# Attention and mixture-of-LoRA block on one core: half of the probability tiles turned by VectorE squares and SBUF to SBUF DMAs instead of TensorE

## The chip, the cores and the metric

The kernel runs on one core of a Trainium2 chip. The metric is device time in microseconds (us) of one execution; lower is better. One execution with the hardware profiler gives the page and the trace that are quoted below.

## The reference

The input `x` has 4 sequences of 512 tokens with 1024 features, all in 32-bit floats. One transformer block is computed:

```python
x = x + layernorm(attention(layernorm(x)))          # 32 query heads, 8 key/value heads, 32 features each
x = x + layernorm(lora_moe(layernorm(x)))           # a dense 1024x1024 layer plus a top-2 mix of 8 LoRA experts

# attention, per head:
scores = q @ k.T / sqrt(32)                         # q, k after rotary embedding
scores = where(causal, scores, -1e20)
out = softmax(scores) @ v                           # then the output projection w_o
```

The change concerns the step between `softmax` and `@ v`. TensorE sums over partitions, so the probabilities, which are computed with queries on the partitions, have to be turned until the keys lie on the partitions.

## The kernel before

The 2048 tokens are cut into 16 tiles of 128 (`Tokens`; `tok.i` is the tile's place, 0 to 3, within its sequence). Dense layers work on pairs of tiles with seven block products in place of eight (`seven`): their weights come from HBM as pieces of 128x512 (`bring_pieces`, line 489) into a ring of `RING = 13` buffers, issued on SP's DMA queue. A piece is requested when the product that last used its buffer is done.

Attention of a tile is cut into groups (`Group`). A group takes four heads side by side on the TensorE array (`QUADS = 4`; `r` is the quadrant) and `n` columns of heads, so that `m = n * (i + 1)` blocks of 128 keys are handled at once: m is 4, 4, 3 and 4 for `i` = 0 to 3, with 2, 4, 8 and 8 groups per tile, 88 groups in all. For each group

- `scores` (TensorE, line 1390) writes all four quadrants to PSUM; VectorE adds the causal mask (line 1459) and takes the maxima (line 1469);
- `quadrant` lets ScalarE take the exponential (line 1411) into the SBUF tile `pr` and GpSimd (POOL) multiply by the reciprocal of the sum (line 1425);
- `turn` (line 1485) turns `pr` with TensorE, m squares of 128x128 per quadrant, into PSUM; `copy` (lines 335 and 336) brings them back to SBUF as `prT`, on ScalarE or VectorE, whichever the planner finds free;
- `values` (line 1508) multiplies `prT` with `v`; the result `av` is copied to `aT`.

The order of instructions on every engine is written out at build time by a planner, the class `Order`. Every piece of work is an `Op` with an estimated duration for each engine that could do it, or a TensorE `Step`; `_choice` picks TensorE's next step among the lanes (scores, turns, values, dense products), and `run` gives the other engines' work out in the planned order of time. The estimates are constants of the source. For DMAs, `sp(us, issue)` is the time that SP's queue is planned to be taken, and `LANDS = 2.8` us is added until the data is there. Once built, each engine keeps its order, and only semaphores delay it. SP's DMAs share eight semaphores in turn, so that an issue also waits for the DMA eight before it.

`Norm.apply` (lines 562 and 568) normalises rows on VectorE or ScalarE, and `load_y` (line 879) brings the residual rows.

Of the kernel before, what the change touches and what calls it, by code (L numbers as in the profile page):

```python
# [11 lines left out]
F32 = mybir.dt.float32  # L12
AF = mybir.ActivationFunctionType
ALU = mybir.AluOpType
AX = mybir.AxisListType

P = 128
# [4 lines left out]
EPS = 1e-5  # L22
MASKED = -1e30
QUADS = P // HD

# [64 lines left out]
class Order:  # L92
# [109 lines left out]
    def _choice(self, scores, values, lanes):  # L202

        later, ready, last = [], [], []
        score = scores[0] if scores else None


        value = values[0] if values and values[0].tiled else None
        waiting = []
        if score is not None and value is not None:  # L210
            if self._comes(score):
                waiting.append(values)
            if self._comes(value) and not self._is_ready(value):
                waiting.append(scores)
        for lane in lanes:
            at = self._ready(lane[0])
            if at is None:
                continue
            later.append(at)
            if at <= self.now:  # L220
                if any(lane is w for w in waiting):
                    last.append(lane)
                elif at + SAFE <= self.now:
                    return lane, None
                else:
                    ready.append(lane)
        if ready or last:
            return (ready + last)[0], None
        what = self._next()
        if what is not None:  # L230
            later.append(max(what[0], self.now + 1e-6))
        if not later:
            raise RuntimeError("TensorE's work cannot go on")
        return None, min(later)
# [31 lines left out]
def kernel(  # L266
# [24 lines left out]
    GL = E + E * R  # L291
    PSUM = bass.MemoryType.PSUM
    QSCALE = 1.0 / math.sqrt(HD)
    BANKS, SOFT, RING = 4, 8, 13

    const = ctx.enter_context(tc.tile_pool(name="const", bufs=1))
    xpool = ctx.enter_context(tc.tile_pool(name="xpool", bufs=1))
# [2 lines left out]
    qpool = ctx.enter_context(tc.tile_pool(name="qpool", bufs=8))  # L300
    kvpool = ctx.enter_context(tc.tile_pool(name="kvpool", bufs=4))
    soft = ctx.enter_context(tc.tile_pool(name="soft", bufs=SOFT))
    weights = ctx.enter_context(tc.tile_pool(name="weights", bufs=RING))
    small = ctx.enter_context(tc.tile_pool(name="small", bufs=2))
    ps_sc = ctx.enter_context(tc.tile_pool(name="ps_sc", bufs=1, space=PSUM))
# [4 lines left out]

    banks = Slots(BANKS)
    soft_slots, part_slots, piece_slots = Slots(SOFT), Slots(4), Slots(RING)
    xnT_slots, aT_slots, hT_slots = Slots(2), Slots(3), Slots(2)
    qT_slots, kT_slots, raw_slots, turn_slots = Slots(8), Slots(4), Slots(6), Slots(1)
    xa_slots, y_slots, w_slots, v_slots = Slots(1), Slots(3), Slots(4), Slots(8)
    order = Order(banks)
    start = order.start

# [12 lines left out]
    def copy(n, out, in_):  # L331

        return Op(
            0,
            act=(0.15 + n * 0.00085, lambda: nc.scalar.copy(out(), in_())),  # L335
            dve=(0.15 + n * 0.00105, lambda: nc.vector.tensor_copy(out(), in_())),  # L336
        )

    def combine(urgent, out, in0, in1, op, engines=("dve", "pool")):
# [155 lines left out]
    class Norm:  # L495
# [60 lines left out]
        def apply(self, dst, src, h):  # L556
            cols = slice(h * 512, (h + 1) * 512)
            yield Op(
                self.urgent,
                dve=(  # L560
                    0.66,
                    lambda: nc.vector.tensor_scalar(
                        dst()[:, cols], src()[:, cols], self.rstd, self.shift, ALU.mult, ALU.add
                    ),
                ),
                act=(
                    0.82,
                    lambda: nc.scalar.activation(  # L568
                        dst()[:, cols], src()[:, cols], AF.Identity, bias=self.shift, scale=self.rstd
                    ),  # L570
                ),
            )
# [299 lines left out]
    def load_y(tok):  # L872

        yield y_slots.take()
        yield has_rest if tok in pairs[0] else all_mixed

        def issue():
            tok.y = xpool.tile([P, D], F32, tag="y", bufs=3, name=f"y_{tok.t}")
            nc.sync.dma_start(out=tok.y, in_=x[tok.t * P : (tok.t + 1) * P, :])

        yield sp(P * D * 4 / 1024 / RATE, issue)
        yield LANDS
        tok.has_y.finish(order.at)
# [487 lines left out]
    class Group:  # L1371
        def __init__(self, tok, at, n):
            self.tok, self.seq, self.at, self.n = tok, tok.seq, at, n
            self.kt = at // GROUP
            self.name = f"{tok.t}_{at}"
            self.parts = 2
            self.exps, self.normed = [Task() for _ in range(QUADS)], [Task() for _ in range(QUADS)]
            self.rtot = [Task() for _ in range(QUADS // 2)]
            self.pr, self.prT = [None] * QUADS, [None] * QUADS
            self.has_prT = [Task() for _ in range(QUADS)]  # L1380

    def scores(g):

# [17 lines left out]

        def quadrant(r):
            urgent = 1 + r / QUADS
            yield soft_slots.take()
            pr = soft.tile([P, GROUP, P], F32, tag="soft", name=f"pr_{g.name}_{r}")
            pr = g.pr[r] = pr.rearrange("p a b -> p (a b)")
            for c in range(g.n):
                yield act(
                    0.5 + n * 0.00079,
                    urgent,  # L1410
                    lambda: nc.scalar.activation(  # L1411
                        pr[:, c * n : (c + 1) * n],
                        sc4[:, r, c, :],
                        AF.Exp,
                        bias=nmax[:, r, c : c + 1],
                        accum_out=total[:, r, c : c + 1],
                    ),
                )
            g.exps[r].finish(order.at)
            yield g.rtot[r // 2]  # L1420
            for c in range(g.n):
                yield pool(
                    0.33 + n * 0.00089,
                    urgent,
                    lambda: nc.gpsimd.tensor_scalar(  # L1425
                        pr[:, c * n : (c + 1) * n],
                        pr[:, c * n : (c + 1) * n],
                        rtot[:, r, c : c + 1],
                        1.0,
                        ALU.mult,  # L1430
                        ALU.mult,
                    ),
                )
# [42 lines left out]
        start(softmax(), order.now)  # L1476
        for h in range(QUADS // 2):
            start(totals(h), order.now)

    def turn(g, r):  # L1480

# [16 lines left out]
    def values(g):  # L1498
# [5 lines left out]
        for c in range(g.n):  # L1504
            for j in range(i + 1):
                for r in range(QUADS):
# [1 line left out]
                    nc.tensor.matmul(  # L1508
                        av[r * HD : (r + 1) * HD, c, :],
                        lhsT=g.seq.v[j][:, head * HD : (head + 1) * HD],  # L1510
                        rhs=g.prT[r][:, c * (i + 1) + j, :],
                        start=(j == 0),
                        stop=(j == i),
                    )

        def end():
            yield g.valued.done
            for r in range(QUADS):
                soft_slots.give(order.at)
            yield copy(  # L1520
                g.n * P, lambda: tok.aT[:, g.at : g.at + g.n, :], lambda: av[:, : g.n, :]
            )
# [83 lines left out]
    for k, g in enumerate(groups):  # L1606
# [4 lines left out]
        if k > 1:  # L1611
# [2 lines left out]
        g.turned = [  # L1614

            Step(0.109 * blocks, partial(turn, g, r), [g.normed[r | 1]], bank=True, turns=True)
            for r in range(QUADS)
        ]
        needs = [tok.seq.has_v[i] for i in range(tok.i + 1)] + [tok.aT_taken]
        g.valued = Step(0.218 * blocks, partial(values, g), needs, bank=True, soon=g.has_prT)  # L1620
# [133 lines left out]
```

## Time and profile before

| | us |
|---|---|
| median of 3 runs | 1164.1 (1162.73 to 1164.26) |
| profiled execution, its own time | 1164.45 |
| its span, first to last instruction | 1162.7 |
| granted TensorE clock | 0.996 of full speed |

| engine | busy us | instructions |
|---|---|---|
| TensorE, matmuls (PE) | 1136.4 | 7240 |
| TensorE, weight loads (PEld) | 624.5 | 7240 |
| VectorE (DVE) | 832.6 | 1629 |
| ScalarE (ACT) | 530.1 | 1545 |
| GpSimd (POOL) | 611.7 | 859 |

The span is the time from the first to the last instruction on the core. The chain of waits follows the work back from the last instruction, at each step to what released it, and is the view that tells which engine sets the end. Busy time of PE alone says little, for matmuls overlap. Issuing a DMA does not count as busy time: SP's queue (SPq) has rows of its own in the timeline. The DMA queue moved 230.12 MB in 117632 packets, and its packets took 60.7% of the time of 16 DMA engines.

### The profile page before, as it was taken

What the parts mean: (1) busy time and instruction counts of PE and PEld (TensorE: products, weight loads), DVE (VectorE), ACT (ScalarE), POOL (GpSimd) and SP (SyncE); (2) the same over time, 40 slices, a digit from 0 to 9 for tenths busy, and PEclk for the clock granted to TensorE, in tenths of its full rate; (3) what the DMA queues carried; (4) which work ended last, traced back from release to release, by engine and by line L of the source; (5) the groups of instructions that cost most, each with busy time, mean ns of one, the idle gap of its engine ahead of it and who ended that gap; (6) DMA issues with size and microseconds to landing.
All of it is one profiled execution on the core that took longest, in us unless ns stands there. A gap on an engine that the chain in (4) does not pass through costs nothing.

```text
span 1162.7 us, 21371 instructions
## 1 busy us (share of the span) xinstructions
PE 1136.4 (98%) x7240; PEld 624.5 (54%) x7240; DVE 832.6 (72%) x1629; ACT 530.1 (46%) x1545; POOL 611.7 (53%) x859
## 2 busy tenths in 40 slices
PE   7999999999999999999999999999999999999997
PEld 3455554655556455565555555456555555556443
DVE  4787767987678756787667876768866787668564
ACT  0354554555555355555434434455644555454010
POOL 2686856743756435544555253654545564547231
PEclk9999999999999999999999999999999999999999
DMA  9879777563773637625477443673457745585783
GB/s 349 277 255 310 248 253 263 170 220 97 257 239 96 199 109 253 192 83 176 141 244 256 137 135 118 219 229 106 149 168 233 243 135 160 164 268 187 221 285 118
DMA packets 117740, 231.48 MB, mean 199 GB/s; under 512 B 13440, under 2 KB 14464, under 8 KB 117632
## 3 DMA queue, kind: packets, MB, share of 16 engines
q1 hardware_dynamic: 117632, 230.12, 60.7%
q8 instruction: 58, 0.95, 0.3%
q14 instruction: 50, 0.41, 0.1%
HBM read 209.09 MB, written 20.97 MB: 198 GB/s over the span
## 4 chain that ended last, share of the span: by engine, by line
PE 86%; DVE 7%; DMA 3%; POOL 1%; ACT 1%; issue 1%; SPq 0%; POOLq 0%; ACTq 0%
PE acc_f L618 18%; PE acc_o L618 16%; PE acc_q L618 14%; PE pt_p L1485 11%; PE acc_kv L618 8%; PE sc L1390 7%; PE av L1508 6%; PE acc_gl L618 2%; DVE nmax L1469 2%; PE pt_xn L593 1%; PE pt_h L593 1%; DMA piece<-in_w_qkv_dram 1%; ACT pr L1411 1%; PE pt_q L1010 1%; DMA xa<-in_x_dram 1%
## 5 line engine op out<-in xcount | busy, mean ns | idle before, releaser
L1425 POOL TENSOR_SCALAR pr<-pr,rtot 128x256 f32<-128x256 f32 (+3 forms) x512 | 300.5, 602 | 251.9 <-DVE rtot L1440 183.3
L1411 ACT ACTIVATE pr<-sc,nmax 128x256 f32<-128x256 f32 (+3 forms) x512 | 265.0, 536 | 121.8 <-DVE nmax L1469 63.6
L1469 DVE TENSOR_REDUCE nmax<-sc 128x2 f32<-128x768 f32 (+3 forms) x176 | 198.2, 1126 | 33.7 <-ACT pr L1411 30.6
L1485 PEld LDWEIGHTS pt_p<-ident,pr 128*128 128x128 f32 x1280 | 144.5, 141 | 59.3 <-issue 49.1
L1485 PE MATMUL pt_p<-ident,pr 128*128 128x128 f32 x1280 | 173.2, 276 | 2.4 <-DVE raw_q L727 1.0
L335 ACT COPY prT<-pt_p 128x512 f32<-128x512 f32 (+1 forms) x261 | 134.1, 548 | 62.4 <-PE pt_p L1485 61.0
L1459 DVE TENSOR_TENSOR sc<-sc,cmask 128x256 f32<-128x256 f32 (+2 forms) x176 | 96.7, 550 | 48.6 <-PE sc L1390 39.0
L335 ACT COPY aT<-av 128x128 f32<-128x128 f32 (+2 forms) x83 | 26.1, 315 | 222.1 <-PE av L1508 222.0
L618 PE MATMUL acc_f<-piece,s_f 128*128 128x512 f32 x256 | 120.1, 602 | 2.1 <-DVE s_f L343 2.1
L618 PE MATMUL acc_kv<-wkv_sb,T_xn 128*128 128x512 f32 x256 | 119.4, 597 | 0.0
L1411 ACT ACTIVATION_READ_ACCUMULATOR pr<-sc,nmax 128x1 f32 x512 | 108.3, 212 | 0.0
L618 PE MATMUL acc_o<-piece,aT 128*128 128x512 f32 x232 | 105.9, 594 | 0.0
L618 PE MATMUL acc_q<-piece,s_q 128*128 128x512 f32 x224 | 105.4, 595 | 0.1
L618 PE MATMUL acc_q<-piece,T_xn 128*128 128x512 f32 x224 | 103.9, 594 | 0.1
L618 PE MATMUL acc_o<-piece,s_o 128*128 128x512 f32 x224 | 102.8, 593 | 0.0
L1390 PE MATMUL sc<-kT,qT 32*128 32x384 f32 (+3 forms) x1024 | 93.9, 464 | 0.5 <-ACT pr L1411 0.5
L1508 PEld LDWEIGHTS av<-prT,v 128*32 128x32 f32 x2560 | 64.8, 109 | 50.1 <-issue 35.0
L618 PE MATMUL acc_f<-piece,T_h 128*128 128x512 f32 x192 | 90.0, 592 | 0.0
L343 POOL TENSOR_TENSOR y<-y,w 128x512 f32<-128x512 f32 x61 | 79.1, 1309 | 20.3 <-ACT w L568 14.9
L1508 PE MATMUL av<-prT,v 128*32 128x128 f32 x2560 | 88.7, 276 | 0.2 <-DVE prT L336 0.2
L336 DVE COPY prT<-pt_p 128x512 f32<-128x512 f32 (+1 forms) x91 | 58.3, 642 | 31.3 <-PE pt_p L1485 29.7
L541 POOL TENSOR_TENSOR rstd<-veps,neg_half 128x1 f32<-128x1 f32 x64 | 35.0, 549 | 86.1 <-DVE veps L537 85.8
(154 smaller groups left out, 1416.3 us busy)
## 6 DMA issues: line engine op xcount, KB each, us to landing
piece<-mixed_f SPq DMA_DIRECT2D x128, 256.0 KB, 3.5
piece<-in_w_o_dram SPq DMA_DIRECT2D x116, 256.0 KB, 3.6
piece<-mixed_q SPq DMA_DIRECT2D x112, 256.0 KB, 3.4
piece<-mixed_o SPq DMA_DIRECT2D x112, 256.0 KB, 4.1
piece<-in_w_qkv_dram SPq DMA_DIRECT2D x100, 256.0 KB, 3.7
piece<-in_w_base_dram SPq DMA_DIRECT2D x96, 256.0 KB, 3.3
xa<-in_x_dram SPq DMA_DIRECT2D x32, 256.0 KB, 3.8
y<-in_x_dram SPq DMA_DIRECT2D x16, 512.0 KB, 5.7
```

Of the source, the lines that this page charges most:

```text
L335: act=(0.15 + n * 0.00085, lambda: nc.scalar.copy(out(), in_())),
L336: dve=(0.15 + n * 0.00105, lambda: nc.vector.tensor_copy(out(), in_())),
L343: engine.tensor_tensor(out=out(), in0=in0(), in1=in1(), op=op)
L541: nc.gpsimd.tensor_tensor(out=self.rstd, in0=self.veps, in1=neg_half, op=ALU.pow)
L618: nc.tensor.matmul(acc[0][:, :n], lhsT=lhsT(c), rhs=w(c), start=(c == 0), stop=last)
L1390: nc.tensor.matmul(sc[:, r, c * n : (c + 1) * n], lhsT=tok.qT[g.kt][rows, (g.at + c) % GROUP, :], rhs=seq.kT[g.kt][rows, :n], start=True, ...
L1411: lambda: nc.scalar.activation(pr[:, c * n : (c + 1) * n], sc4[:, r, c, :], AF.Exp, bias=nmax[:, r, c : c + 1], accum_out=total[:, r, c : ...
L1425: lambda: nc.gpsimd.tensor_scalar(pr[:, c * n : (c + 1) * n], pr[:, c * n : (c + 1) * n], rtot[:, r, c : c + 1], 1.0, ALU.mult, ALU.mult,),
L1459: lambda: nc.vector.tensor_tensor(out=diag, in0=diag, in1=cmask.unsqueeze(1).unsqueeze(1).to_broadcast([P, q, g.n, P]), op=ALU.add,),
L1469: lambda: nc.vector.tensor_reduce(nmax[:, some, : g.n], sc4[:, some], AX.X, ALU.max, negate=True),
L1485: nc.tensor.transpose(pt[:, j, :], g.pr[r][:, j * P : (j + 1) * P], ident)
L1508: nc.tensor.matmul(av[r * HD : (r + 1) * HD, c, :], lhsT=g.seq.v[j][:, head * HD : (head + 1) * HD], rhs=g.prT[r][:, c * (i + 1) + j, :], ...
```

## The change

Quadrants 0 and 1 (`TURNED = 2`) are turned as before. For quadrants 2 and 3 ScalarE writes the exponentials into a tile `pair` in which each row is cut into strips of 32 columns; VectorE turns every square of 32x32 in place with one instruction per group; 16 DMAs from SBUF to SBUF, each of 32 partitions, move the 4x4 grid of squares to their turned places in the tile `flat`; `values` reads `flat` for those quadrants. The planner is told 0.07 us of SP's queue for each of the 16.

Beside it, `copy` and `Norm.apply` go to ScalarE alone; the rings are smaller (`RING` 13 to 9, `SOFT` 8 to 6, `y` 3 to 2) to make room for two `pair` and two `flat` tiles; and one rule of `_choice`, which held scores back while values were about to come, is gone.

```diff
-            if self._comes(value) and not self._is_ready(value):
-                waiting.append(scores)
...
-    BANKS, SOFT, RING = 4, 8, 13
+    BANKS, SOFT, RING = 4, 6, 9
+    PAIRS, FLATS = 2, 2
+    SIDE = 32
+    NS = P // SIDE
...
     def copy(n, out, in_):
...
             act=(0.15 + n * 0.00085, lambda: nc.scalar.copy(out(), in_())),
-            dve=(0.15 + n * 0.00105, lambda: nc.vector.tensor_copy(out(), in_())),
...
         def apply(self, dst, src, h):
...
-                dve=(
-                    0.66,
-                    lambda: nc.vector.tensor_scalar(
-                        dst()[:, cols], src()[:, cols], self.rstd, self.shift, ALU.mult, ALU.add
-                    ),
-                ),
...
-            tok.y = xpool.tile([P, D], F32, tag="y", bufs=3, name=f"y_{tok.t}")
+            tok.y = xpool.tile([P, D], F32, tag="y", bufs=2, name=f"y_{tok.t}")
...
         def quadrant(r):
+            if r < TURNED:
+                yield soft_slots.take()
+                pr = soft.tile([P, GROUP, P], F32, tag="soft", name=f"pr_{g.name}_{r}")
+                pr = g.pr[r] = pr.rearrange("p a b -> p (a b)")
+                to = [pr[:, c * n : (c + 1) * n] for c in range(g.n)]
+                exp_in = [sc4[:, r, c, :] for c in range(g.n)]
+                exp_out = to
+            else:
+                yield g.has_pair
+                j = tok.i + 1
+                strips = g.pair[:, :, r - TURNED]
+                to = [strips[:, :, c * j : (c + 1) * j, :] for c in range(g.n)]
+                exp_in = [
+                    sc4[:, r, c, :].rearrange("p (j s k) -> p j s k", s=NS, k=SIDE)
+                    for c in range(g.n)
+                ]
+                exp_out = [a.rearrange("p s j k -> p j s k") for a in to]
...
+    def flip(g):
+        m = g.n * (g.tok.i + 1)
+        q = QUADS - TURNED
+        yield pair_slots.take()
+        g.pair = flips.tile([P, NS, q, m, SIDE], F32, tag="pair", bufs=PAIRS, name=f"pair_{g.name}")
+        g.has_pair.finish(order.at)
+        yield g.normed[TURNED:]
+        flat_pair = g.pair.rearrange("p s r m k -> p (s r m k)")
+        yield dve(
+            0.1 + NS * q * m * SIDE * 0.00105,
+            1,
+            lambda: nc.vector.transpose(out=flat_pair, in_=flat_pair),
+        )
+        yield flat_slots.take()
+        g.flat = flips.tile([P, NS, q, m, SIDE], F32, tag="flat", bufs=FLATS, name=f"flat_{g.name}")
+
+        def move():
+            for a in range(NS):
+                for b in range(NS):
+                    nc.sync.dma_start(
+                        out=g.flat[b * SIDE : (b + 1) * SIDE, a],
+                        in_=g.pair[a * SIDE : (a + 1) * SIDE, b],
+                    )
+
+        yield sp(NS * NS * 0.07, move, -1)
+        yield LANDS
+        pair_slots.give(order.at)
+        for r in range(TURNED, QUADS):
+            g.has_prT[r].finish(order.at)
...
     def values(g):
-                        rhs=g.prT[r][:, c * (i + 1) + j, :],
+                        rhs=(
+                            g.prT[r][:, c * (i + 1) + j, :]
+                            if r < TURNED
+                            else g.flat[:, :, r - TURNED, c * (i + 1) + j, :]
+                        ),
...
         g.turned = [
             Step(0.109 * blocks, partial(turn, g, r), [g.normed[r | 1]], bank=True, turns=True)
-            for r in range(QUADS)
+            for r in range(TURNED)
         ]
```

## The prediction

> **What bounds the kernel now.** I read the page's first section, then the chain that ended last, then that chain piece by piece in a stretch of dense work, then the waits and the issue rows of the DMA queue, since the change adds most of its instructions there.
>
> ```profile
> PE 1136.4 (98%) x7240; PEld 624.5 (54%) x7240; DVE 832.6 (72%) x1629; ACT 530.1 (46%) x1545; POOL 611.7 (53%) x859
> ...
> PE 86%; DVE 7%; DMA 3%; POOL 1%; ACT 1%; issue 1%; SPq 0%; POOLq 0%; ACTq 0%
> PE acc_f L618 18%; PE acc_o L618 16%; PE acc_q L618 14%; PE pt_p L1485 11%; PE acc_kv L618 8%; PE sc L1390 7%; PE av L1508 6%; PE acc_gl L618 2%; DVE nmax L1469 2%; PE pt_xn L593 1%; PE pt_h L593 1%; DMA piece<-in_w_qkv_dram 1%; ACT pr L1411 1%; PE pt_q L1010 1%; DMA xa<-in_x_dram 1%
> ```
>
> TensorE carries 86% of the chain; 11% is the turning of probabilities (pt_p). SP (SPq) carries nothing.
>
> ```profile
> 581.93 1.08 PE sc L1390 x16
> 583.01 1.01 PE av L1508 x32
> 584.02 1.02 PE pt_p L1485 x8
> 585.04 0.86 PE acc_f L618 x2
> 585.90 0.88 PE pt_p L1485 x8
> 586.78 6.87 PE acc_f L618 x16
> ```
>
> One group (four heads side by side on the array) is 1.08 us of scores, 1.01 of values and four turns of four squares, 0.44 each; everything else is dense products, 0.86 us for each 512-column product (two instructions).
>
> ```profile
> SPq L489 <- PE acc_q L618: 231.7, 167, 20.6
> SPq L489 <- PE acc_f L618: 224.2, 184, 10.9
> SPq L489 <- PE acc_o L618: 142.7, 174, 6.3
> ```
>
> Most of SP's waits are weight pieces waiting for TensorE to free a buffer: the queue runs ahead of its consumer and has time to spare.
>
> **What the change removes from TensorE.** Of 1280 squares, 640 stay. In the chain eight squares take 0.88 us, 0.11 each, so 640 x 0.11 = 70 us leave the engine that sets the end. The profiled execution took 1164.45 us around a span of 1162.7 and lies 0.35 us over the median of 1164.1. If nothing took the place of the squares: 1164.45 - 70 = 1094.
>
> **What it moves between VectorE and ScalarE.** VectorE loses its share of the copies (prT 58 us, T_h 14, kT 3, T_xn 10, lowT 2) and of the normalising passes (18 + 10 + 10): 126 us. It gains 88 square transposes of 1024 or 768 elements per partition. No row shows one; the nearest are the reductions over as many elements, 1.22 and 0.96 us: 56 x 1.22 + 32 x 0.96 = 99 us. As no row is a transpose I keep half of that and twice that as bounds, 50 and 200 us, and take 99, by the row; even 200 leaves VectorE at 900 us of work in a run that can't be under 1094. ScalarE loses 176 of the 352 prT copies and takes all that remain: 176 x about 0.55 = 97 us in place of 134, plus T_xn, T_h, kT and lowT (27 us) and 58 normalising passes of 0.81 (47 us): about +37 us, 49% busy. Both stay below TensorE, whose dense products cover them; without that cover they'd be worth tens of us at most. The exponentials and POOL's multiplications write the same elements in runs of 32; between nothing and 10% of 565 us on engines that are half idle, I take nothing.
>
> **What it adds to SP's queue.** Each of the 88 groups issues 16 DMAs of 32 partitions (24 or 32 KB): 1408 beside the 808 of before. They need a price per issue, and the planner in the kernel says 0.07 us (`sp(NS * NS * 0.07, ...)`). The trace's rows:
>
> ```profile
> 1.69 3.95 SPq L392 DMA_DIRECT2D wkv_sb<-in_w_qkv_dram  x8
> 5.96 0.33 SPq L489 DMA_DIRECT2D piece<-in_w_qkv_dram  x1
> 6.73 0.33 SPq L392 DMA_DIRECT2D bqkv_sb<-in_b_qkv_dram  x1
> 7.37 0.33 SPq L489 DMA_DIRECT2D piece<-in_w_qkv_dram  x1
> ...
> 11.38 0.33 SPq L489 DMA_DIRECT2D piece<-in_w_qkv_dram  x1
> ...
> L489 SPq DMA_DIRECT2D piece<-mixed_f x128: 319/320/853, 234.2 to 1141.2; - x128
> ...
> L879 SPq DMA_DIRECT2D y<-in_x_dram x16: 328/333/497, 19.3 to 1111.1; - x16
> DMA to landing us min/median/max: 2.0/4.7/8.9
> ```
>
> The busy time of an issue is never under 0.319 us, whether it moves 256 or 512 KB. Eight issues with hardly a wait take 3.95 us: (3.95 - 0.43) / 7 = 0.50 from start to start. From 5.96 to 11.38 eight steps take 5.42 us, 0.68 each, and there every issue waits for the landing of the DMA eight before it. In the instruction order of the changed kernel each of the sixteen waits so too. Here a rule stands against a row: the Trainium skill's page "DMA: Bandwidth & Descriptors", section "Anatomy of one DMA — SWDGE (gpsimd) path", gives the sequencer's dispatch as about 50 ns and puts the cost into some 2 us of completion. By that rule sixteen issues are 0.8 us, which is the planner's view; by the rows they are 16 x 0.33 = 5.3 to 16 x 0.68 = 10.9 us. The rows decide. I take 0.60, just over the middle of 0.50 and 0.68: each flip DMA has that wait, but what it waits for lands sooner than the wkv_sb loads waited for there (median 5.0 us). That is 9.6 us a group. Landing: the shortest in the trace is 2.0 us (y, out_dram), 2.7 for xa; I take 2.2. The same page's rule table ("Rules for kernel authors") speaks against transfers under 64 KB as mostly overhead; that is this case.
>
> **What waits behind it.** The first of the sixteen waits for VectorE's transpose; weight pieces queue behind it on SP. The values of a group on TensorE wait for the last of the sixteen; dense products queue behind them, for TensorE's order is fixed at build time. The planner put the values where sixteen issues of 0.07 and a landing of 2.8 end, some 4 us after the transpose. I counted in the changed kernel's order, for each group, the TensorE work from the last TensorE instruction that SP must have seen before it can issue the sixteen to the group's values, priced by the rows above: median 7.4 us, a quarter of the groups under 5.9, a quarter over 10.9. What is needed is 0.5 (a weight piece between) + 9.6 + 2.2 = 12.3 us. TensorE idles for the difference. Summed over the 24 groups of the first and second token block of a sequence (18 are short) this is 96 us; over the 64 of the third and fourth (52 short) 260 us. These 64 have a second bound: in each of four stretches SP issues some 256 flips and 104 others, 256 x 0.60 + 104 x 0.50 = 206 us, where TensorE has about 130 us of work, also by count: 76 x 4 = 302 us. The larger counts: 96 + 302 = 398.
>
> The smaller buffers go with this. Pieces drop from 13 to 9: 9 x 0.86 = 7.7 us of dense work against a landing of 3.6, free as long as SP is free, and inside the 302 us where it isn't. The two pair buffers are held from exponentials to landing, some 20 us, 10 per group, under SP's 13 per group, so nothing more. Soft 8 to 6 and y 3 to 2 follow fewer turned tiles and cost nothing that I can see beside those stalls. The dropped rule (scores wait for ready values) lets scores go alone: the trace pairs them to save TensorE time, PAIRED is 0.46 us, so 88 x 0 to 0.46 bounds it at 40 us; I take nothing, since a stalled TensorE hides it. DMA engines: a 2 KB packet takes 0.607 x 16 x 1162.7 / 117632 = 96 ns, so 45056 more packets of half the size take 48 to 96 ns each, 135 to 270 us over 16 engines, on top of 706: busy but not the bound.
>
> Sum: 1094 + 398 = 1492; predicted 1495.
>
> **Rivals.**
> 1. SP issues at the pace of a free run, 0.50. Need 0.5 + 8.0 + 2.2 = 10.7: 69 us for the first 24 groups; SP 180 against 130 us in the four stretches, 200 us: 1094 + 269 = 1363. For it: a small DMA lands early, so the wait for the eighth before may be over. Against it: the flips go between SBUF and SBUF over 32 partitions, a form that no row shows, and pieces of 256 KB share the rings. Between 0.33 and 0.45 it is 1180 to 1300.
> 2. Faster. The sequencer takes a small DMA as cheaply as planned: at 0.07 the need is 3.8 us, 5 us are short in all, 1099. The point from which it decides: the stalls equal the 70 us gained at a need of about 7.45, which is 0.31 us an issue. Below that it is faster. No issue in the trace is below 0.319.
> 3. Worse than forecast: 0.68 and a landing of 2.7 need 14.1 us: 129 + 4 x (226 - 130) = 513, so 1607; above 0.70, or with flips queued behind pieces on the DMA engines (landing 5 us), over 1640.
> That the change doesn't halve the squares is out: its order holds 640 of them.
>
> **How the numbers follow.** Forecast (0.55 to 0.70 an issue, 1430 to 1640): 0.60. Rival 1 near 0.50 (1270 to 1430): 0.22; its low end (1170 to 1270): 0.07. Rival 3 above 1640: 0.05. Faster: 0.05; the same: 0.01. About 0.2% is what a measurement of this kernel can tell from no change. The range 1270 to 1640 leaves out 0.18.
>
> **What would show it.** Right: 640 squares at L1533; a DMA row of 1408 flat<-pair issues with busy time over 0.3 us and starts 0.5 to 0.7 apart; TensorE's busy share near 70 to 75%; av<-flat at the head of the waits, for hundreds of us, released by DMA; SPq in the chain; DVE transposes near 1.2 us; ScalarE near 50%. Wrong: flips less than 0.35 us apart, TensorE over 90% busy, or PEld waiting for ScalarE's copies or POOL in place of DMA.

## The result, and the profile after

| | before | after |
|---|---|---|
| median of 4 runs, us | 1164.2 (1162.7 to 1165.0) | 1756.8 (1752.0 to 1761.3) |
| ratio to before, 95% interval | | 1.509 (1.505 to 1.514) |
| span of the profiled execution, us | 1162.7 | 1759.6 |
| granted TensorE clock | 0.996 | 0.844 |

The change costs 593 us. The forecast was 1495 us with a range up to 1640: the direction was right, the size was not. From the page of the changed kernel, the busy times, the granted clock in 40 slices, and the chain that ended last by engine and by line:

```profile
PE 1271.0 (72%) x6600; PEld 666.7 (38%) x6600; DVE 796.7 (45%) x1496; ACT 557.5 (32%) x1581; POOL 612.1 (35%) x868
...
PEclk9886678898978988788988988888888789887898
...
SPq 36%; PE 28%; DMA 23%; issue 5%; DVE 4%; ACT 2%; POOL 1%; ACTq 0%; DVEq 0%; POOLq 0%
SPq L1517 34%; DMA flat<-pair 7%; PE acc_f L616 6%; PE av L1556 5%; PE acc_o L616 4%; PE acc_q L616 4%; DMA piece<-mixed_o 3%; PE pt_p L1533 3%; DMA piece<-mixed_q 2%; PE acc_kv L616 2%; DMA piece<-in_w_o_dram 2%; DMA piece<-mixed_f 2%; SPq
```

TensorE fell from 98% to 72% busy, and yet its busy time grew from 1136 to 1271 us although 640 squares left it: part of its work ran at half clock. SP's queue, which carried nothing of the chain before, carries 36% of it, nearly all by the sixteen transfers of line 1517. The chain from 905 to 927 us (start, us, what) shows how one group follows the other:

```profile
905.56 6.18 DMA piece<-in_w_o_dram
911.76 0.51 SPq L1517
912.31 0.59 SPq L1517
...
916.12 0.59 SPq L1517
916.70 0.04 issue
916.75 1.88 DMA flat<-pair
...
918.67 1.86 PE av L1556 x27
920.52 5.78 DMA piece<-mixed_o
926.33 0.51 SPq L1517
```

From 911.76 on these are the eighth to the fifteenth issue of one burst, 0.63 us from start to start. Then comes the sixteenth, 1.88 us from its start to its landing, then the values that waited for it, then a weight piece that the end of the values let SP ask for; its landing, 5.78 us, is what the eighth issue of the next burst waits for, for SP's transfers share eight semaphores in turn. The values of this group take 1.86 us, where a group took 1.01 before. SP's own timeline a little later:

```profile
944.96 10.01 SPq L1517 DMA_DIRECT2D flat<-pair  x16
955.07 1.00 SPq L493 DMA_DIRECT2D piece<-mixed_q  x2
```

and TensorE's in the same microseconds (start, us, what, and in brackets how long it had been idle and what ended that):

```profile
949.85 0.41 PE L1556 MATMUL av<-prT,v 128*32 128x128 f32 x4
956.57 0.43 PE L1556 MATMUL av<-flat,v 128*32 128x128 f32 x2 [6.30 <-DMA flat<-pair]
...
958.41 4.78 PE L616 MATMUL acc_q<-piece,s_q 128*128 128x512 f32 x6
...
964.33 1.88 PE L616 MATMUL acc_q<-piece,T_xn 128*128 128x512 f32 x4
```

TensorE stands for 6.30 us until the sixteenth transfer has landed. The six product instructions after the values take 0.80 us each in the mean, the four at 964.33 take 0.47. The same microseconds as stretches (from and to, length, busy us of each engine with instructions, granted clock, share of the DMA engines, GB/s):

```profile
950.30:955.50 5.20, 0.00 (x0) 0.00 (x0) 0.35 (x1) 0.00 (x0) 0.98 (x3) 1.00 0.20 51
955.60:962.30 6.70, 5.73 (x33) 3.31 (x34) 0.00 (x0) 2.49 (x4) 1.91 (x2) 0.50 0.88 286
962.40:966.00 3.60, 3.60 (x12) 1.67 (x11) 1.47 (x3) 1.29 (x2) 0.48 (x1) 1.00 0.68 206
```

The clock is halved shortly before the wait ends and stays so for some 6.7 us. The rows of the tile that is moved (busy ns min/median/max), and the waits of all engines and of SP's queue (us in total, times, longest):

```profile
L1517 SPq DMA_DIRECT2D flat<-pair x1408: 507/588/1891, 54.4 to 1647.7; - x176
...
L1509 DVE STREAM_TRANSPOSE pair<-pair x88: 923/1233/1247, 53.1 to 1635.2; 128x1024 f32<-128x1024 f32 x56, 128x768 f32<-128x768 f32 x32
...
DMA to landing us min/median/max: 1.7/1.8/7.2
```

```profile
ACT aT L340 <- PE av L1556: 599.0, 84, 14.3
...
PE av L1556 <- DMA flat<-pair: 367.6, 69, 10.4
```

```profile
SPq L493 <- PE acc_f L616: 122.5, 77, 14.3
SPq L493 <- PE acc_q L616: 102.1, 71, 12.3
SPq L493 <- PE acc_o L616: 59.4, 63, 5.4
```

TensorE waits for SP's transfers, and SP for buffers that TensorE frees: 284 us in these three rows. Neither is busy all the time, because each is in order behind the other. Last, the four stretches of the prediction, from the first flip of a sequence's third tile to the first flip after its fourth, in the same columns:

```profile
184.70:457.20 272.50, 184.92 (x1068) 100.01 (x1061) 125.87 (x230) 92.81 (x273) 106.74 (x132) 0.82 0.48 153
567.80:845.40 277.60, 207.64 (x1145) 108.51 (x1146) 131.47 (x247) 92.45 (x261) 92.67 (x126) 0.86 0.46 141
988.60:1258.30 269.70, 190.39 (x1027) 98.09 (x1025) 120.95 (x231) 87.37 (x228) 84.97 (x117) 0.85 0.42 128
1331.80:1608.80 277.00, 195.05 (x1041) 99.86 (x1040) 120.65 (x215) 83.30 (x230) 88.58 (x119) 0.82 0.48 149
sum 1096.80, PE 777.99 PEld 406.48 DVE 498.94 ACT 355.93 POOL 372.96; mean PE 194.50 PEld 101.62 DVE 124.73 ACT 88.98 POOL 93.24
```

They take 274 us each where the prediction had 206. Summed over the four, SP's queue waits 59 us a stretch by its own list of waits: 37 for TensorE, 12 for the landing of earlier transfers, 8 for VectorE.

### The profile page after: what moved, and what is told of

It reads as the page before. It is cut to its first block, busy times and chain, and to the rows that moved or that the text cites. A ratio compares the mean times of both kernels' runs of the same rounds, so it can differ in the third digit from the quotient of the medians.

```text
span 1759.6 us, 22332 instructions
## 1 busy us (share of the span) xinstructions
PE 1271.0 (72%) x6600; PEld 666.7 (38%) x6600; DVE 796.7 (45%) x1496; ACT 557.5 (32%) x1581; POOL 612.1 (35%) x868
## 4 chain that ended last, share of the span: by engine, by line
SPq 36%; PE 28%; DMA 23%; issue 5%; DVE 4%; ACT 2%; POOL 1%; ACTq 0%; DVEq 0%; POOLq 0%
SPq L1517 34%; DMA flat<-pair 7%; PE acc_f L616 6%; PE av L1556 5%; PE acc_o L616 4%; PE acc_q L616 4%; DMA piece<-mixed_o 3%; PE pt_p L1533 3%; DMA piece<-mixed_q 2%; PE acc_kv L616 2%; DMA piece<-in_w_o_dram 2%; DMA piece<-mixed_f 2%; SPq L493 2%; DMA piece<-in_w_base_dram 2%; DMA out_dram<-y 1%
## 5 line engine op out<-in xcount | busy, mean ns | idle before, releaser
L1556 PE MATMUL av<-flat,v 128*32 128x128 f32 x1280 | 134.0, 374 | 372.7 <-DMA flat<-pair 367.6
L1440 POOL TENSOR_SCALAR pr<-pr,rtot 128x128 f32<-128x128 f32 (+3 forms) x256 | 152.5, 609 | 490.6 <-DVE rtot L1455 357.9
L1556 PEld LDWEIGHTS av<-flat,v 128*32 128x32 f32 x1280 | 99.1, 148 | 391.6 <-issue 326.6
L1426 ACT ACTIVATE pr<-sc,nmax 128x128 f32<-128x128 f32 (+3 forms) x256 | 133.7, 530 | 172.1 <-DVE sc L1474 113.6
L1440 POOL TENSOR_SCALAR pair<-pair,rtot 128x128 f32<-128x128 f32 (+3 forms) x256 | 143.3, 573 | 73.9 <-DVE rtot L1455 63.2
L1426 ACT ACTIVATE pair<-sc,nmax 128x128 f32<-128x128 f32 (+3 forms) x256 | 132.9, 540 | 20.4 <-DMA flat<-pair 20.4
L1556 PE MATMUL av<-prT,v 128*32 128x128 f32 x1280 | 136.6, 352 | 0.4 <-ACT prT L340 0.4
L1533 PE MATMUL pt_p<-ident,pr 128*128 128x128 f32 x640 | 128.0, 353 | 4.8 <-ACT prT L340 2.4
L1533 PEld LDWEIGHTS pt_p<-ident,pr 128*128 128x128 f32 x640 | 99.5, 183 | 52.7 <-issue 40.4
L1509 DVE STREAM_TRANSPOSE pair<-pair 128x1024 f32<-128x1024 f32 (+1 forms) x88 | 100.2, 1139 | 10.2 <-POOL pair L1440 6.7
```

What stands on the lines that cost most here:

```text
L1426: lambda: nc.scalar.activation(exp_out[c], exp_in[c], AF.Exp, bias=nmax[:, r, c : c + 1], accum_out=total[:, r, c : c + 1],),
L1440: lambda: nc.gpsimd.tensor_scalar(to[c], to[c], rtot[:, r, c : c + 1], 1.0, ALU.mult, ALU.mult,),
L1509: lambda: nc.vector.transpose(out=flat_pair, in_=flat_pair),
L1533: nc.tensor.transpose(pt[:, j, :], g.pr[r][:, j * P : (j + 1) * P], ident)
L1556: nc.tensor.matmul(av[r * HD : (r + 1) * HD, c, :], lhsT=g.seq.v[j][:, head * HD : (head + 1) * HD], rhs=(g.prT[r][:, c * (i + 1) + j, :] ...
```

## Experiments

Times are single executions; those of before beside them lay between 1161.6 and 1164.5 us, and a few us are not read.

**Is it the number of issues?** The first run leaves the DMAs out and keeps all side edits (e1). Two others (e2, e3) move the same bytes in fewer transfers that leave the strips at their old places, so that the values come out of misplaced probabilities; e18 moves half the bytes in as many transfers.

```diff
e1_sides
-TURNED = 2
+TURNED = 4
-    BANKS, SOFT, RING = 4, 6, 9
+    BANKS, SOFT, RING = 4, 8, 9
e2_four: for a in range(NS)
+                nc.sync.dma_start(out=g.flat[:, a], in_=g.pair[:, a])
e3_eight: for a in range(NS), h in range(2)
+                    nc.sync.dma_start(out=g.flat[half, a], in_=g.pair[half, a])
e18_three9
-TURNED = 2
+TURNED = 3
-    BANKS, SOFT, RING = 4, 6, 9
+    BANKS, SOFT, RING = 4, 7, 9
```

> The changed kernel with TURNED = 4: all squares on TensorE again, no flips, no DMAs between SBUF tiles; everything else of the change stays (copies and normalising on ScalarE alone, ring of 9, two y buffers, scores no longer held back); SOFT is 8 again, which four turned quadrants need. Theory A (the loss is SP's queue: sixteen issues of 0.63 us a group, and TensorE idle behind them) and theory B (on top of A, TensorE's granted clock falls to half after such stalls and makes its own work dearer by about 200 us) both expect what stood before, 1150 to 1185 us, clock over 0.98. Theory C (the edits beside the flips cost a good part) expects over 1220.

Measured: 1181.5 us, 18 more than before.

> The changed kernel with the sixteen DMAs of 32 partitions replaced by four of 128 partitions, which move the same bytes but leave the squares in their strips (so the values are computed from misplaced probabilities); the order of everything else is the same. Need of a group: 4 x 0.634 + 0.5 + 1.8 = 4.8 us, short by 8 us over all groups. A: 1094 + 8, some 1100 to 1125, clock near 1. B: the same, for without stalls the clock stays. C, or the strided reading of flat by the values: over 1170 even with the queue free.

Measured: 1182.2 us. That is outside the expected 1100 to 1125: TensorE is idle for 80 us where e1 had 42, with a landing of 2.8 us where 1.8 was reckoned, and the granted clock is 0.977. So what the squares gave is lost again with four issues already. Its page and its four stretches:

```profile
PE 1100.2 (93%) x6600; PEld 565.1 (48%) x6600; DVE 795.4 (67%) x1496; ACT 553.9 (47%) x1581; POOL 616.7 (52%) x868
```

```profile
sum 682.70, PE 653.41 PEld 332.59 DVE 499.73 ACT 349.56 POOL 379.39; mean PE 163.35 PEld 83.15 DVE 124.93 ACT 87.39 POOL 94.85
```

> As with four DMAs, but eight of 64 partitions (squares left in their strips again). Need: 8 x 0.634 + 0.5 + 1.8 = 7.4 us; by the count of the prediction 68 us short in all. A: 1094 + 68 = 1162 (1150 to 1190). B: the stalls are 1 to 2 us long; if the clock falls for those too, 1200 to 1260 and a granted clock under 0.95; if it needs longer idling, as A. A queue that costs by bytes or by rows and not by issues would leave it at the time of sixteen.

Measured: 1312.9 us, over the expected range too. From four issues to eight, 352 issues cost 131 us, 0.37 each; from eight to sixteen, 704 cost 444 us, 0.63 each. That is the pace at which SP issues them: in sum, beyond eight nothing covers one.

> The changed kernel with one quadrant turned by VectorE and DMAs instead of two (TURNED = 3, SOFT 7, RING 9): the same sixteen issues per group, each with half the bytes, and 960 squares on TensorE. A and D, issues decide and not bytes: 1757 + 320 x 0.11 = 1790 us, some 1750 to 1800 us. If the bytes or the packets decide: half of the loss goes, 1450 to 1500 us. It is also the base of the next run.

Measured: 1727.3 us, 23 us under A's range and far above 1500. Half the bytes at the same number of issues bring 30 us, with 35 us of squares more on TensorE. The issues decide, and the bytes count for little.

**Which side edit costs the 18 us?** One edit at a time in the kernel before: the rule of `_choice` dropped (e11), `copy` and `Norm.apply` on ScalarE alone (e12), `RING = 9` (e16).

> The kernel before with one edit: the rule that holds scores back while values are about to come is gone. The side edits together cost 18 us. C1, this rule is most of it (scores no longer pair with values; the prediction bounded it at 40 us and took nothing): 1172 to 1185 us. C2, it is the smaller rings and ScalarE's copies: 1163 to 1168 us.

> The kernel before with one edit: copies and normalising passes go to ScalarE alone. C2, ScalarE as the only engine for copies makes TensorE's turns wait for their buffers: 1170 to 1180 us. C1, the copies lie beside the products as the prediction said: 1162 to 1168 us.

> The kernel before with one edit: RING 13 to 9. Of the 18 us of the side edits the dropped rule gave 6 and ScalarE's copies nothing. C3, the ring is the rest: 1170 to 1177 us. Without bursts in the queue 9 pieces are enough: 1161 to 1165 us.

Measured: 1167.7 (before beside it 1161.6), 1161.2 and 1179.8 us (before 1163.2). The rule costs about 6 us, little over the scatter, ScalarE nothing, the ring about 16. Why a ring of nine costs so much without bursts stays open: TensorE is busy 9 us longer there and hardly waits longer for pieces; the planner's order changed with the ring. The smaller `SOFT` and the two `y` buffers were not tried alone.

**Is the half clock on the path?** Dummy products ahead of a group's values keep TensorE busy while it would wait: six for every group (e4), or for 68 groups as many as its stall was counted to hold (e9).

```diff
+        for w in range(WARM):                       # e9: WARM.get(g.name, 0), 0 to 9
+            nc.tensor.matmul(av, lhsT=ident, rhs=wkv_sb[:, w % ND, :], start=True, stop=True)
```

> The changed kernel with six needless products of 512 columns on TensorE ahead of each group's values, into the same PSUM tile, which the first real product then overwrites: 88 x 6 x 0.86 = 454 us of work more, put where TensorE now waits for the DMAs. A alone (the time is the stalls'): no gain, 1757 or up to 100 us more, since where a stall is shorter than 5.2 us the products delay the values. B: the clock stays near 1 and the work that now runs at half speed (about 200 us of loss) runs at full speed: 1540 to 1650 us although TensorE does more, granted clock over 0.95.

Measured: 1765.0 us. 88 x 6 x 0.86 = 454 us of added work cost 8 us: TensorE isn't the bound. As products also stood before groups that had no stall, the clock's part can't be read from it.

> Ahead of a group's values go dummy products, only as many as fit into the stall that the trace of the changed kernel showed for that group (384 in all, 0 to 9 for a group, some 330 us of TensorE work at 128x512 in groups that waited anyway). A, the queue alone sets the end: the products lie in the waits, so the time stays at 1740 to 1790 us whatever the clock does. B, the lowered clock is on the path: the products keep TensorE busy, the granted clock rises from 0.84 to above 0.95, and most of the 174 us that the half clock takes from TensorE's work comes back: 1550 to 1650 us.

Measured: 1718.5 us. The answer on clocks for this run and for the changed kernel:

```profile
core 0: 1716.8 us, clock 0.935
```

```profile
core 0: 1759.6 us, clock 0.844
```

At 0.844 of full clock some (1 - 0.844) / 0.5 x 1760 = 549 us pass at half speed, and the same TensorE work takes 1271 us where it took 1100 in e2. In e9 it is (1 - 0.935) / 0.5 x 1717 = 223 us, three fifths less, and the time falls by 38 us. That lies in neither range: A had at most 17, B 107 to 207. So the half clock is on the path, but with the smaller part of these 171 us (1271 - 1100): most of the slow work seems to lie in time that TensorE would have waited. What the rest of the half clock costs, and how far the added products themselves held values back, was not tried; in proportion the whole would be 38 x 549 / 326 = 64 us, an estimate.

**The queue, or the values' wait?** In e10 SP issues the sixteen transfers at the same places, but from a tile that doesn't change into tiles that nobody reads; all squares go over TensorE. In e20 the reverse: the transfers and the values' wait stay, and the weight pieces leave SP's queue (664 by the trace, where the expectation says 692); the products read a resident weight, so that the sums are others of the same size.

```diff
e10_unread (TURNED = 4)
+        yield g.normed[2:]
+        flat = flips.tile([P, NS, q, m, SIDE], F32, tag="flat", bufs=FLATS, name=f"flat_{g.name}")
...
+                        out=flat[b * SIDE : (b + 1) * SIDE, a],
+                        in_=still[a * SIDE : (a + 1) * SIDE, b, :, :m],
...
+        yield sp(NS * NS * 0.07, move, -1)
e20_nopieces
-                piece.sb = weights.tile([P, 512], F32, tag="piece", name=f"piece_{k}")
-                nc.sync.dma_start(out=piece.sb, in_=piece.in_)
+                piece.sb = wkv_sb[:, k % ND, :]
```

> All squares are turned by TensorE again, as in the run with the side edits alone (1181.5 us). At the changed kernel's places SP issues the same sixteen transfers of 32 partitions per group, from a tile that never changes into tiles that nobody reads: VectorE's transposes are left out, and neither SP waits for them nor TensorE for the landing. A, SP's issues are the bound by themselves: 1408 x 0.634 us and 808 others at about 0.5 us are some 1300 us; since the weight pieces wait in the same queue behind them, the time is 1300 to 1400 us. A+, it is the loop (values wait for the flips, the flips behind pieces, the pieces for buffers that TensorE frees): without the values' wait the loop is cut, the rest is A, so of the 575 us between 1181.5 and 1757 a part of 120 to 220 us is the queue alone and the remainder, over 350 us, the loop. If the queue alone did everything, this kernel would be near 1700 us.

Measured: 1626.0 us, over A's range. What ended TensorE's idle time ahead of instructions that use a piece (us, times; a weight load and its matmul can both stand in it), what SP's queue waited for, and the four stretches:

```profile
  DMA piece<-mixed_o: 127.8, 51
  DMA piece<-in_w_o_dram: 102.4, 45
  DMA piece<-mixed_q: 79.4, 30
  DMA piece<-in_w_qkv_dram: 63.6, 31
```

```profile
SPq L495 <- PE acc_f L618: 64.2, 75, 14.4
SPq L495 <- PE acc_q L618: 53.3, 52, 8.4
...
SPq L1508 <- DMA piece<-mixed_o: 17.6, 46, 1.5
```

```profile
sum 1015.30, PE 776.14 PEld 405.70 DVE 449.16 ACT 399.45 POOL 360.88; mean PE 194.03 PEld 101.43 DVE 112.29 ACT 99.86 POOL 90.22
```

Nobody reads a transfer, and 444 us are lost against e1: TensorE now waits for weight pieces that stand behind the bursts. SP waits too, 33 us a stretch: 18 for landings of earlier transfers (the first eight issues of a burst can each wait for one, and a weight piece lands only 4.4 to 5.5 us after its issue) and 15 for buffers that TensorE frees. The theory that the loop through the values' wait holds most of the loss (A+) falls. The obvious next one was the ring: a burst of 10.1 us outlasts nine pieces of 0.86 us.

```diff
e14_ring13 (e10 with)
-    BANKS, SOFT, RING = 4, 8, 9
+    BANKS, SOFT, RING = 4, 8, 13
e19_three12 (e18 with)
-    BANKS, SOFT, RING = 4, 7, 9
+    BANKS, SOFT, RING = 4, 7, 12
```

> As the run whose sixteen transfers nobody reads (1626 us), with 13 buffers for weight pieces in place of 9; for room the transfers read wkv_sb and write one tile. D, a burst of sixteen holds the weight pieces back for 10.1 us and a landing (some 4 us) while the ring holds 9 x 0.86 = 7.7 us of products, so that TensorE runs dry in every burst: four more pieces are 3.4 us per group, 88 x 3.4 = 300 us, and the time falls to 1300 to 1420 us, near the 1300 us that SP's issues add up to. A, throughput of the queue alone: nothing changes, 1590 to 1640 us.

> As the run before it, with 12 buffers for weight pieces in place of 9 (the smaller tiles leave room). D: three more pieces let SP and TensorE run 2.6 us further apart, for pieces behind a burst and for bursts behind a piece alike: up to 88 x 2.6 = 230 us less than with 9. A, the queue's throughput alone: within 30 us of the run with 9.

Measured: 1630.8 us, no change, and 1689.0, 38 us less than e18. (For room the transfers of e14 read `wkv_sb` and write a single tile.) The ring falls as the main cause as well. That a larger one only shifts the moment at which TensorE runs dry would fit both runs, but is not shown.

> The changed kernel with the weight pieces left out of SP's queue: 692 loads are not issued, and the products read slices of a resident weight (wkv_sb) in their place, so the sums are other sums of the same size. TensorE's order is the same instruction for instruction, and so are the sixteen transfers of each group and the values that wait for them. E, the loop through SP's order (flips behind pieces, pieces behind buffers that TensorE frees after the values): SP has only 893 us of flips and some 55 us of others left, never waits for TensorE's buffers, and the bursts run ahead: 1250 to 1350 us. F, the latency of a group's own sixteen issues and its landing, 12 us against 4 us planned, is enough: 1600 to 1700 us. In between: the share of each is read off.

Measured: 1530.9 us, between E and F. Its waits, first of all engines, then of SP's queue, and its four stretches:

```profile
PE av L1555 <- DMA flat<-pair: 262.8, 59, 8.6
...
PEld av L1555 <- DMA flat<-pair: 88.2, 20, 9.1
```

```profile
SPq L1516 <- DVE pair L1508: 234.7, 39, 18.1
```

```profile
sum 924.90, PE 725.94 PEld 381.07 DVE 495.65 ACT 350.41 POOL 376.30; mean PE 181.48 PEld 95.27 DVE 123.91 ACT 87.60 POOL 94.08
```

Without the pieces SP no longer waits for TensorE's buffers but for the next group's transposes, and the values wait on. (144 other transfers stay in the queue, the input rows among them, and so does the pace of the sixteen.) Against a floor of 1181.5 - 70 = 1112 us, which is e1 less the prediction's price of the squares, an estimate, the values' wait costs 419 us without the pieces, the queue 444 us without the values' wait, both together 645. Neither is the cause alone, and they overlap by 419 + 444 - 645 = 218 us, a difference in which the floor cancels. The two `pair` and two `flat` tiles were not varied; in the changed kernel ScalarE waited 20 us in all for a `pair` tile to come free.

**Can the planner, a second queue or another way repair it?** e5 tells the planner the measured price, `sp(NS * NS * 0.634, move, -1)`. e6 issues every second transfer on ScalarE's queue. e8 sends the strips to DRAM in one transfer of 128 partitions and back in four; e21 and e13 tell the planner the landings of e8 and plan to give the `pair` tile back when the store has landed, and e13 also undoes the side edits on the rule, `copy` and `Norm.apply`.

```diff
e6_queues
-                    nc.sync.dma_start(
+                    (nc.sync, nc.scalar)[b % 2].dma_start(
e8_bounce
+            nc.sync.dma_start(out=there, in_=flat_pair)
...
+            for b in range(NS):
+                nc.sync.dma_start(out=to[b * SIDE : (b + 1) * SIDE], in_=cut[:, :, b])
...
+        yield sp(0.5, store, -1)
+        yield 3.0
+        yield sp(NS * 0.5, bring, -1)
e21_landing (e8 with)
-        yield 3.0
+        yield 5.0
...
-        yield LANDS
+        yield LANDS + 2.0
```

> Only the figure that the planner is told for the sixteen transfers of a group changes, from 1.12 us to 10.14 us (16 x 0.634 us, the pace seen in the changed kernel); no instruction is added or removed, the order moves. A, SP's queue can't issue more: 88 groups x 16 x 0.634 us are 893 us, the other 808 transfers at some 0.5 us 400 us, 1290 us in all, so the time can't fall below about 1300 us; it comes to 1300 to 1450 us, since a part of the order still leaves SP idle. A', the loss is in the order alone (groups placed as if their squares were there after 4 us): the time falls to 1200 to 1300 us. If neither, it stays at 1700 to 1760 us. In both A and A' the granted clock rises above 0.9, since the stalls get fewer.

Measured: 1800.7 us; both theories miss. The values wait less at the head of the list (274 us where it was 368), and TensorE's idle time ahead of products of one layer, weight loads counted too, grew from 11 to 223 us:

```profile
PE av L1556 <- DMA flat<-pair: 274.2, 59, 7.5
...
  DMA piece<-mixed_f: 223.0, 30
```

With the true price a part of the wait moved from the values to the pieces.

> Of the sixteen transfers of a group every second one is issued on ScalarE's queue, the order stays. A, the pace of one queue: each queue has eight issues of a group, so a group's squares are there some 5 us earlier; at the 0.63 us per issue that the step from eight to sixteen showed, the time falls by up to 704 x 0.63 = 444 us, to about 1310 us, as with eight transfers. A'', the pace is that of the transfers themselves (their descriptors, whoever issues them): the time stays within 60 us of 1757 us. Against A: the ScalarE instructions behind the issues (the copies of values, exponentials) wait up to 8 x 0.6 us, which may give 50 to 150 us back, so 1310 to 1460 us.

Measured: 1593.4 us, 163 less than with one queue and 133 more than the expected range. ScalarE now stands for `pair` tiles that the transfers still hold, where it had waited 20 us before:

```profile
ACT pair L1426 <- DMA flat<-pair: 182.6, 34, 9.1
```

The Trainium skill's "DMA: Bandwidth & Descriptors", "Rules for kernel authors", says that spreading DMAs over engines only saves sequencer issue time. Here exactly that was short; by the row above, a part of what it saved went into ScalarE's waits.

> The turned strips of a group go out to DRAM in one transfer and come back in four, instead of sixteen from SBUF to SBUF: five issues in place of sixteen, and 3 us planned between. A, SP's issues decide: five issues are about the four of the run with 128 partitions to a transfer (1182 us), plus one issue of 0.37 us for 88 groups, 33 us, so 1190 to 1260 us; the second landing lies beside other work, since the planner is told of it. B, the landing decides and not the issues: two landings of 2 us or more in a row, with the wait of SP for the first one ahead of other issues, 88 x 2 to 4 us, so 1360 to 1530 us.

Measured: 1247.7 us, in A's range. The way to the values now has two landings. The row of the four loads, then that of the store:

```profile
L1523 SPq DMA_DIRECT2D flat<-there x352: 303/424/1517, 58.9 to 1134.4; - x176
L1517 SPq DMA_DIRECT2D there<-pair x88: 319/327/832, 54.3 to 1128.4; - x88
```

Five issues cost 136 us over 1112 where sixteen cost 645.

> The run with the way over DRAM (five issues, 1248 us) with the side edits undone (the rule is back, copies and normalising passes may go to VectorE again) and with the planner told the landings that the trace of that run showed (5.0 us until the store is there, 4.8 us for the loads). A and C: 18 us from the side edits and some 40 of the 53 us in which values waited for the landing come back, 1180 to 1200 us. If the squares' 70 us count in full and nothing waits, it is as low as 1120 us, and this would be a version that beats both. If it stays at 1235 to 1250 us, the wait was not in the planner's figures.

> The way over DRAM (1248 us) with one half of what the run at 1355 us changed: the planner is told the landings as measured (5.0 us until the store is there, 4.8 us for the loads), the side edits stay as in the changed kernel. If the told landings were what hurt there, as the told issue price did (1801 us): 1320 to 1370 us. If it was the rule that came back (scores held while values are about to come): 1210 to 1250 us.

Measured: 1354.9 and 1249.1 us. The told landings alone change nothing, so the 106 us come with the edits that were undone, the rule or the copies; which of them was not tried. No version with transfers between the tiles is faster than the kernel before.

## Why the prediction was wrong in size

Its steps, in its order:

- **Squares, VectorE, ScalarE: right.** 640 squares remain at line 1533. The transposes took 100.2 us in sum (88 x 1139 ns) where 99 were taken from the reductions; ScalarE was busy 557.5 us, forecast some 567. The sign "ScalarE near 50%" did not fit the forecast itself, for 567 of 1495 us are 38%; 32% were measured.
- **Price of an issue: somewhat low.** It is 0.634 us from start to start, and 0.667 in the mean of the 88 bursts with the waits for earlier landings, which the prediction's 0.60 was to include. The landing is 1.8 us against 2.2, so that a burst takes 11.9 us from its first issue to its last landing, where 9.6 + 2.2 = 11.8 were forecast. The figure of about 50 ns of dispatch, which the prediction weighed from "DMA: Bandwidth & Descriptors", was rightly set aside: it stands there for GpSimd's path, and an issue holds SP's queue for 0.588 us. The flips stand at the head of TensorE's DMA waits as forecast. TensorE's 72% are as forecast too, but in part by luck: without the half clock, which was not in the sum, 1100 of 1760 us would be 63%.
- **Edits costed at nothing: 18 us.** The ring was called free as long as SP is free; in the kernel before it costs some 16 us with SP free.
- **The clock: not in the sum.** TensorE at half speed for some 549 us was not thought of; taking away three fifths of that gained 38 us.
- **The step that failed: "The larger counts".** For the third and fourth tiles two counts were made, the values' wait and SP's throughput, and only the larger was taken, as if the one filled the time of the other and SP never stood. Over the whole kernel each of the two alone costs more, 419 (e20) and 444 us (e10), than the 398 that were forecast for all stalls, and together they cost 645. Per stretch:

| us per stretch | predicted | measured |
|---|---|---|
| TensorE's work | 130 | 163 (e2, busy) |
| values' wait alone | 130 + 260/4 = 195 | 231 (e20) |
| queue alone | 206 | 254 (e10) |
| both | 206, the larger | 274 |

The wait that was counted for the values, 65 us a stretch, is about right in sum: with TensorE's work as measured it gives 163 + 65 = 228, and e20 has 231. The queue's count is not right. Its issues come to 256 x 0.667 + 112 x 0.50 (the prediction's figure) = 227 us with the waits for landings. In the other 47 of 274 us SP, the supposed bound, stands: it waits 37 us for buffers that TensorE frees and 8 for VectorE, while TensorE waits for SP. Most of the miss appears already when nobody reads the transfers: the queue alone takes 48 us more than its 206 (e10), and SP stands for 33 us there too. Had the larger of the two measured counts been taken, another 20 us would still be missing.

Outside the stretches the prediction had 1492 - 4 x 206 = 668 us and 663 were measured. That is luck, two errors that cancel: TensorE's work there was put at 1094 - 4 x 130 = 574, and is 1112 - 653 = 459 by e2's stretches; the stalls at 96, and the rest over the work is 663 - 459 = 204. So of the 247 us by which all stalls were forecast too small (645 - 398), some 140 lie in the four stretches, 4 x (274 - 163) where 302 were forecast, and 108 outside. There TensorE waits 110 us for the transfers, near the 96; how the half clock and other waits share the remainder stays open.

Rival 1 (0.50 an issue) and the faster rival fell with the price. (The latter's turning point, a need of 7.45 us, is (7.45 - 0.5 - 2.2) / 16 = 0.30 us an issue, not 0.31; nothing hangs on it.) Rival 3 named a size nearer the truth, 1607 and above. Its 0.68 was close to the pace with the waits, its landing of 2.7 was not, and its sum takes the larger count in the same way.

## What to carry to other kernels

When two engines run in fixed orders and each waits for the other, don't take the larger of their two sums: each of them also stands while it waits for the other. A way to reckon it, not tried here, is to price one lap of the loop (issue, landing, work, freed buffer) and to let only work that is queued ahead on both sides cover it. Count DMA issues as an engine's instructions, by a row of the same kind; cutting a group's transfers from sixteen to five, of a kind that holds the queue 0.33 to 0.42 us and not 0.59, was worth 509 us, while the true price in the planner (44 us slower) or a larger ring (5 slower, 38 faster) changed little. A TensorE that waits also slows down, but look whether the slow work lies in the wait's shadow before charging it.

## What the hardware showed that was not expected

- An SBUF to SBUF transfer holds the issuing queue for about 0.59 us whether it spans 32, 64 or 128 partitions (medians 588, 594 and 593 ns), while a store of 128 partitions to DRAM takes 327 and a load of 32 partitions from DRAM 424 (e8). With two queues issuing (e6), three quarters of the time both at once, it is 589 on SP's and 602 on ScalarE's, so that the second queue did not slow the first. In these runs the price goes with the kind of transfer, and not with its partitions or bytes.
- Landing grows with the partitions that a transfer spans, and not simply with its bytes: 1.8 us for 32 partitions (24 and 32 KB), 2.5 and 2.2 for 64 (48 and 64 KB, e3), 2.9 and 2.8 for 128 (96 and 128 KB, e2).
- After a wait of 6.30 us TensorE ran at half clock (0.50 granted from 955.6 to 962.3) for the values and most of the next six product instructions; for the first 5.2 us of the wait full clock was still granted. That fits the Trainium skill's "TensorE: Matmul & The Clock Gate", section "The HAM clock gate", where an idle window of some 3.4 us or more halves the clock. Charged in full it would be some 171 us (1271 - 1100); taking three fifths of the half-speed time away gained 38.
